# Edge batches of five tiles instead of four, partial sums in one go, and another order of the loads at the start

## The chip, the cores and the metric

The kernel runs on one core of a Trainium2 chip. The metric is the time of one execution on the device in microseconds. A core has five engines with queues of their own, which wait for one another only by semaphores: TensorE (PE in the profile; its weight loads are PEld), VectorE (DVE), ScalarE (ACT), GpSimd (POOL) and SyncE (SP). Transfers are issued by SP, ACT and POOL.

## What is computed

One message-passing layer on a graph of 1250 nodes and 40000 edges, sorted by destination, then a residual and a layer norm. Cut to what matters:

```python
x_j = x[src]; v_j = x_j[:, :384].reshape(E, 128, 3); s_j = x_j[:, 384:]
s_j = silu(s_j @ W1 + b1) @ W3 + b3
edge_basis = rbf * cutoff @ W2 + b2            # 20 waves of the edge's length
s1, s2, s3 = split(s_j * edge_basis)
msg = concat([v_j * s1[:, :, None] + s3[:, :, None] * edge_attr[:, None, :], s2])
x = x + segment_sum(msg, dst)                  # first pass
x_j = x[src]
v = U(v_j); v_V = V(v); h = silu(concat([norm(v_V), s_j]) @ Wu1 + bu1) @ Wu2 + bu2
msg = concat([v * s1, sum(v * s1 * v_V) + s3])
x = x + segment_sum(msg, dst)                  # second pass
out = layernorm(x_in + x)
```

In the second pass a message depends on the source node alone. So the kernel does it by nodes, with a matrix of counts (how many edges go from one node to another) in place of a second gather.

## The kernel before

**Tiles.** 128 edges are a tile; there are 313, in 80 batches (`batches`, `NT`): 76 of four tiles, then one of three and three of two. The edges stand in chunks of 512; four chunks make a group (`NGR` = 20), and a batch holds the same quarter of the four chunks of its group, so that the four tiles go to four different windows of 32 destination nodes.

**The head** (`gnn_resnorm`, L85 to L413). Node features are loaded in pieces: the scalar part by ACT's queue, the vector part by POOL's, small weights and the edges' fields by SP's. `turn_s`, `inner_layer` and `make_rows` make the ten blocks of `table1` (PE and ACT make the products, DVE multiplies the features in `table_row`, L611, SP stores the row, L616). The edges' fields are turned by PE (`by_tile`, L293). Then DVE checks by two reductions (L371) that every edge lies in its chunk's window; PE adds up the misses (L377), and all engines read the number and branch into `windowed` (L415, L416).

**The main loop** (`windowed`, the loop over `t` at L1730). A step `t` does, in this order of issue: `messages(t)`, in which DVE multiplies the gathered rows by the edge factors `eb` (L938, L940), makes `hot` (L870) and `spread` (L881) from columns that lie in `eb` too, runs the tasks of `amid`, and compares places in `make_pair` (L958); then the tasks of `first`; `add_messages(t-1)`, in which PE sums the messages into the group's bank `agg` (L974, L980); `count_links(t-1)` (PE, L1003); the tasks of `early`; `edge_factors(t+1)`, in which PE writes the next factors into `eb` (L928); `gather(t+3)`, one indirect DMA on POOL for each tile (L769), of which the first waits for these factors; then the tasks of `mid`, `late` and `dve`. Each engine works through its part of this order; it is written out by hand. There is one set of `eb`, so that the factors of a batch can be written only when DVE's `spread` has read those of the batch before. PSUM's banks are shared out so: four are `eb`, and one each is `agg`, `adj` (counts), `begun`, and `work`, which all short works share.

**The second pass** is worked into the same steps. A block of 128 nodes has its sums after eight steps (`begins`); its update takes ten steps more (`links_at`). From then on its rows can be multiplied by counts. A chain (b, begin, end) in `chains` is the part of output block b that comes from source blocks begin to end-1. `begin_out` does one source block per call (two matmuls of 512 columns, L1378), and the calls are spread over `early` and `late` tasks by `slots`. The sum stays in the bank `begun` until `copy_begun` takes it out (ACT, L1397). `cast_counts` makes the counts for a chain beforehand.

Of the kernel before, what the change touches and what calls it, by code (L numbers as in the profile page):

```python
# [11 lines left out]
F32 = mybir.dt.float32  # L12
# [34 lines left out]
PACK = 4096.0  # L47

# [16 lines left out]
def gnn_resnorm(  # L65
# [43 lines left out]
    )  # L109
    sh.n_nodes, sh.width, sh.n_edges, sh.NB, sh.tail = n_nodes, width, n_edges, NB, tail  # L110
# [22 lines left out]
    def load_edges(t, ap, per=1):  # L133

        flat = ap if per == 1 else ap.rearrange("e k -> (e k)")
        n = full * CHUNK * per
        nc.sync.dma_start(t[:full, :], flat[:n].rearrange("(c e) -> c e", e=CHUNK * per))
        if rest:
            nc.sync.dma_start(
                t[full : full + 1, : rest * per], flat[n:].rearrange("(o e) -> o e", o=1)  # L140
            )
# [9 lines left out]
    def load(engine, ap, shape, name):  # L151
        t = const.tile(shape, F32, name=name)
        engine.dma_start(t, ap)
        return t
# [15 lines left out]
    sh.nodes = const.tile([P, NB * width], F32, name="nodes")  # L170
# [12 lines left out]
    nc.gpsimd.memset(sh.src_r[unfilled:, :], 0.0)  # L183

    size = CPG * (V + 2 * C)
    sh.more = const.tile([P, 3 * size], F32, name="more")
# [20 lines left out]
    sh.b1_sb = load(nc.sync, b1.rearrange("(p o) -> p o", o=1), [C, 1], "b1_sb")  # L207
# [3 lines left out]
    sh.w3_sb = load(nc.sync, w3, [C, V], "w3_sb")  # L211
    load_outer(nc.sync, of_s)
    load_edges(dst_r, dst)
    load_edges(sh.src_r.bitcast(I32), src)


# [10 lines left out]

    row_i = front.tile([P, 1], I32)
    nc.vector.tensor_copy(row_i, part)
    nc.vector.tensor_scalar(row_i, row_i, -WIN, None, op0=ALU.bitwise_and)  # L230
    place = front.tile([P, 3], F32)
    nc.vector.tensor_copy(place[:, 2:3], row_i)
    place_row = front.tile([P, 1], F32, name="place_row")
    nc.vector.tensor_copy(place_row, row_i)
    nc.vector.scalar_tensor_tensor(
        place[:, 0:1], place[:, 2:3], float(SHARE - WIN) / WIN, part, op0=ALU.mult, op1=ALU.add
    )
    nc.vector.tensor_scalar(
        place[:, 2:3], place[:, 0:1], float(P - GSPAN), float(-P), op0=ALU.is_ge, op1=ALU.mult
    )  # L240
    nc.vector.scalar_tensor_tensor(
        place[:, 1:2], place[:, 0:1], float(GSPAN), place[:, 2:3], op0=ALU.add, op1=ALU.add
    )
    nc.gpsimd.memset(sh.wgt_r[unfilled:, :], 1.0)
    lane = numbers([P, P], [[1, P]], 0, 0, "lane")
    nc.vector.tensor_sub(place[:, 2:3], part, place_row)
    nc.vector.tensor_scalar(
        place[:, 2:3], place[:, 2:3], float(-N_RBF - 1), None, op0=ALU.add
    )
    nc.gpsimd.tensor_scalar(  # L250
        w2_sb[:, V:], lane[:, :CARRY], place[:, 2:3], None, op0=ALU.is_equal
    )
    half_n = numbers([P, N_RBF], [[1, N_RBF]], 1, 0, "half_n")
# [3 lines left out]

    nc.gpsimd.tensor_scalar(half_n, half_n, 0.5, None, op0=ALU.mult)
    sh.sel = const.tile([P, 2, P], F32, name="sel")
    for k in range(2):  # L260
        nc.gpsimd.tensor_scalar(sh.sel[:, k, :], lane, place[:, k : k + 1], None, op0=ALU.is_equal)

# [4 lines left out]
    )  # L267
    sh.basis = const.tile([P, TPC * CPG, FEAT], F32, name="basis")
# [80 lines left out]
    inner_layer(first_s[:, 2 * P :], (3, 4))  # L349
    part_bias(nc.vector, bias_f, slice(0, V))  # L350


    local_r = front.tile([NCP, CHUNK], F32)
# [1820 lines left out]
```

## Time and profile before

| | |
|---|---|
| Time, median of 3 runs | 478.65 us (477.8 to 480.88) |
| The profiled execution | 480.96 us |
| Its span, first to last instruction | 479.2 us |
| Mean granted clock of TensorE | 0.957 |
| Busy: PE / DVE / ACT / POOL | 402.6 / 427.8 / 375.3 / 334.9 us |
| Moved by DMA | 123.29 MB, 257 GB/s |

Busy time is that of instructions on the engine; issuing a transfer, waiting and branching are not in it. An instruction's duration includes its latency, so that two that follow each other on DVE overlap a little in the records; what one costs its engine is the distance between the starts of two. Matmuls are pipelined, and their ends are modelled. In a row of a timeline, what stands in brackets is the idle time of the engine before it and what ended it; "issue" means that the profile shows nothing else that it waited for.

### The profile page before, as it was taken

What the parts mean: (1) busy time and instruction counts of PE and PEld (TensorE: products, weight loads), DVE (VectorE), ACT (ScalarE), POOL (GpSimd) and SP (SyncE); (2) the same over time, 40 slices, a digit from 0 to 9 for tenths busy, and PEclk for the clock granted to TensorE, in tenths of its full rate; (3) what the DMA queues carried; (4) which work ended last, traced back from release to release, by engine and by line L of the source; (5) the groups of instructions that cost most, each with busy time, mean ns of one, the idle gap of its engine ahead of it and who ended that gap; (6) DMA issues with size and microseconds to landing.
All of it is one profiled execution on the core that took longest, in us unless ns stands there. A gap on an engine that the chain in (4) does not pass through costs nothing. (4 is left out here: it accounts for less than half of the span.)

```text
span 479.2 us, 11259 instructions
## 1 busy us (share of the span) xinstructions
PE 402.6 (84%) x4259; PEld 229.3 (48%) x4259; DVE 427.8 (89%) x675; ACT 375.3 (78%) x971; POOL 334.9 (70%) x364
## 2 busy tenths in 40 slices
PE   8645586878879778798889888989999999999992
PEld 6322243445445345444435544555555655555782
DVE  6569899999999899999999999999999999978584
ACT  4377846689869968877977897799899889967672
POOL 9267777777777777777777777777777777771530
PEclk9857979899999999989989999999999999999998
DMA  8887888788888888888888988888888888879024
GB/s 238 301 247 253 254 265 271 240 279 262 281 254 272 289 259 275 270 269 255 280 276 255 293 267 280 266 291 287 287 275 293 265 284 291 280 242 319 4 71 151
DMA packets 37810, 123.29 MB, mean 257 GB/s; under 512 B 7124, under 2 KB 9782, under 8 KB 37746
## 3 DMA queue, kind: packets, MB, share of 16 engines
q0 software_dynamic: 25568, 104.34, 69.0%
q1 hardware_dynamic: 10834, 17.35, 10.6%
q10 hardware_dynamic: 1344, 0.79, 0.5%
q8 instruction: 35, 0.57, 0.5%
q14 instruction: 29, 0.24, 0.2%
HBM read 112.94 MB, written 9.51 MB: 256 GB/s over the span
## 5 line engine op out<-in xcount | busy, mean ns | idle before, releaser
L769 POOL DMA_INDIRECT more<-table,src_i x189 | 184.6, 977 | 66.3 <-issue 48.1
L769 POOL DMA_INDIRECT nodes<-table,src_i x124 | 119.8, 966 | 37.8 <-issue 33.2
L903 ACT ACTIVATE one<-one,weight,src_f 128x128 f16<-128x128 f16 x313 | 128.5, 482 | 0.2
L928 PE MATMUL eb<-w_sb,basis_t 25*128 25x388 f32 x614 | 74.1, 551 | 54.3 <-DVE spread L881 43.9
L893 ACT ACTIVATE one<-number,low 128x128 f16<-128x128 f16 x313 | 99.8, 392 | 11.2 <-PE adj L1003 11.2
L940 DVE TENSOR_TENSOR more<-more,eb 128x1536 f32<-128x1536 f32 (+2 forms) x48 | 81.8, 1705 | 0.0
L938 DVE TENSOR_TENSOR more<-more,eb 128x1024 f32<-128x1024 f32 (+2 forms) x48 | 57.0, 1190 | 15.0 <-PE eb L928 8.2
L928 PEld LDWEIGHTS eb<-w_sb,basis_t 25*128 25x128 f32 x614 | 24.7, 187 | 76.5 <-DVE spread L881 63.7
L974 PE MATMUL agg<-more,hot 128*32 128x512 f32 x378 | 52.8, 624 | 0.0
L940 DVE TENSOR_TENSOR nodes<-nodes,eb 128x1536 f32<-128x1536 f32 x30 | 52.4, 1747 | 0.0
L980 PEld LDWEIGHTS agg<-more,spread 128*32 128x32 f32 x1134 | 33.5, 111 | 30.2 <-issue 29.6
L938 DVE TENSOR_TENSOR nodes<-nodes,eb 128x1024 f32<-128x1024 f32 x30 | 36.5, 1216 | 6.9 <-PE eb L928 4.0
L881 DVE TENSOR_TENSOR spread<-hot,eb 128x384 f32<-128x384 f32 (+1 forms) x74 | 40.4, 547 | 2.5
L980 PE MATMUL agg<-more,spread 128*32 128x128 f32 x1134 | 40.2, 273 | 0.0
L958 DVE TENSOR_TENSOR pair<-number,column 128x640 f16<-128x640 f16 (+1 forms) x81 | 38.5, 476 | 0.0
L1003 PE MATMUL adj<-pair,one 128*128 128x160 f16 x313 | 35.4, 235 | 0.3 <-DVE basis L827 0.3
L974 PE MATMUL agg<-nodes,hot 128*32 128x512 f32 x248 | 34.9, 619 | 0.0
L980 PEld LDWEIGHTS agg<-nodes,spread 128*32 128x32 f32 x744 | 22.7, 112 | 20.0 <-issue 19.6
L1003 PEld LDWEIGHTS <-one 128*128 128x128 f16 x313 | 21.6, 100 | 16.0 <-issue 13.5
L845 ACT COPY basis_t<-work 128x512 f32<-128x512 f32 x20 | 11.6, 580 | 22.5 <-PE work L840 22.5
L1378 PE MATMUL begun<-upper,cast 128*128 128x512 f32 x57 | 27.8, 487 | 0.0
L980 PE MATMUL agg<-nodes,spread 128*32 128x128 f32 x744 | 27.5, 277 | 0.0
(299 smaller groups left out, 697.3 us busy)
## 6 DMA issues: line engine op xcount, KB each, us to landing
table<-more SPq DMA_DIRECT2D x10, 320.0 KB
more<-table,src_i POOLq DMA_INDIRECT x189, 4.2
spilled<-begun SPq DMA_DIRECT2D x10, 256.0 KB
more<-spilled SPq DMA_DIRECT2D x2, 1280.0 KB
node_x<-in_x_dram SPq DMA_DIRECT2D x35, 64.0 KB
nodes<-table,src_i POOLq DMA_INDIRECT x124, 4.2
out_dram<-more SPq DMA_DIRECT2D x7, 256.0 KB
nodes<-in_x_dram POOLq DMA_DIRECT2D x2, 768.0 KB
```

Source lines behind the costliest of these rows:

```text
L769: got = nc.gpsimd.indirect_dma_start(out=rows_t[:n, j, :], out_offset=None, in_=sh.table1, in_offset=bass.IndirectOffsetOnAxis(ap=sh.src_i ...
L881: nc.vector.tensor_mul(spread[t][:m, js], hots[t][:m, js, None, :].to_broadcast(shape), carried(t, js, m)[:, :, :3, None].to_broadcast(shape),
L893: nc.scalar.activation(onehots[t][:, j, :], number[:, :P], AF.Abs, bias=low[:, e : e + 1])
L903: nc.scalar.activation(one, one, AF.Relu, scale=less[:, e : e + 1], bias=worth[:, e : e + 1])
L928: made = nc.tensor.matmul(made_in[t][:, j, : V + CARRY], turned[g][rows, i, :], sh.w2_sb[rows, :], start=True, stop=True,)
L938: nc.vector.tensor_mul(msg[:m, js, V:], msg[:m, js, V:], factors_of(t, js)[:m, :, C:V])
L940: nc.vector.tensor_mul(msg[:m, js, :V].rearrange("p t (k c) -> p t k c", k=3), msg[:m, js, :V].rearrange("p t (k c) -> p t k c", k=3), fac ...
L958: nc.vector.tensor_tensor(pair[:m, js, :].rearrange("p t (l h) -> p t l h", h=2), number[:m, : PARTS * WIN].rearrange("p (l h) -> p l h", ...
L974: nc.tensor.matmul(agg[j * WIN : (j + 1) * WIN, :], hots[t][:, j, :], msg[:, j, :width], start=(i == 0), stop=False, skip_group_check=True,)
L980: nc.tensor.matmul(agg[j * WIN : (j + 1) * WIN, c * C : (c + 1) * C], spread[t][:, j, c, :], msg[:, j, width:], start=False, stop=(i == la ...
L1003: nc.tensor.matmul(to[:, :, at : at + WIN], one[:m, j, :], pair[:m, j, :].rearrange("e (p n) -> e p n", n=WIN), start=(i == 0 and j == js[ ...
L1378: nc.tensor.matmul(acc, casts[a, b], rows[:, a, :], start=(start and a == first and k == 0), stop=(stop and a == end - 1 and k == 1),)
```

## The change

- **Packs of five.** Gathers, factors and messages work on packs of five tiles (`PACK_OF`, `packs`, `NK` = 65): 60 packs of five, then the tail's batches of four, three, two, two and two. `eb` has five banks. The sums of messages, the counts and all other tasks go on in steps of four tiles; `step_of(s)` gives the pack of a step, so that in steps 5, 10, 15 and so on no new pack begins. Five places of rows stand ready in place of 20 tiles' room; the fifth is a new one (`spare_slots`).
- **Begun sums at one go.** The bank `begun` goes to `eb`. A chain now runs all its blocks in one call, in the bank `work`, in `early` of the step that `steps_of` names (46, 48, 51, 53, 56, 61, 63, 68, 70, 71); the chain of block 8 runs in `late` of step 75. ACT copies it out in the same call.
- **The head.** The vector features go on SP's queue, behind the small weights and `dst`; `src` and `edge_weight` go on POOL's. The inner layer of blocks 5 to 8 comes ahead of the rows. The check of places stands between the rows of blocks 2 and 3, its sum behind row 5 and its copy behind row 6. The attribute load waits for the copy of `src_i` in place of the count. The places' numbers are worked out behind the bias.
- **Turns of the basis.** The tasks of `make_turns`, `make_basis` and `turn_basis` come one to three steps earlier.
- The last two blocks' `upper` and `lower` and the last casts take the spare place when the packs are done (`late_homes`), and `w1`, `w3` lie in the head's own room.

```diff
-    sh.w1_sb = load(nc.sync, w1, [C, C], "w1_sb")
+    sh.w1_sb = load(nc.sync, w1, [C, C], "w1_sb", front)
     load_inner(nc.scalar, of_s, 5)
     nc.scalar.activation(warm, warm, AF.Silu)
-    for b0 in (1, 5):
-        load_inner(nc.gpsimd, slice(0, V), b0)
-    load_outer(nc.gpsimd, slice(0, V))
     ...
-    load_outer(nc.sync, of_s)
-    load_edges(dst_r, dst)
-    load_edges(sh.src_r.bitcast(I32), src)
+    load_edges(nc.sync, dst_r, dst)
+    for b0 in (1, 5):
+        load_inner(nc.sync, slice(0, V), b0)
+    load_outer(nc.sync, slice(0, width))
+    load_edges(nc.gpsimd, sh.src_r.bitcast(I32), src)
+    load_edges(nc.gpsimd, sh.wgt_r, edge_weight)
...
     make_rows((1, 2))
-    inner_layer(next_s, (5, 6, 7, 8))
-    load_edges(sh.wgt_r, edge_weight)
-    make_rows((3, 4))
-    ...
     for k, op in enumerate((ALU.min, ALU.max)):
         nc.vector.tensor_reduce(ends[:, k : k + 1], local_r, AX.X, op)
     ...
+    make_rows((3, 4))
+    rest_s = turn_s((0, 9))
+    make_rows((5,))
+    nc.tensor.matmul(missed, misses, ones[:NCP, 0:1], start=True, stop=True)
+    inner_layer(rest_s, (0, 9))
+    make_rows((6,))
+    nc.vector.tensor_copy(missed_i, missed)
+    make_rows((7, 8, 0, 9))
...
+    def step_of(s):
+        return -(-4 * s // 5) if s < NT - SHORT else s - NT + NK
...
-        def begin_out(chain, a):
+        def begin_out(chain):
             b, begin, end = chain
-            if a == begin:
-                accs[b] = ps_sum.tile([P, BANK], F32, name="begun")
-            products(accs[b], b, a, a + 1, a == begin, a == end - 1)
-            if a == end - 1 and b < NB - 2:
-                copy_begun(b, chain)
+            acc = work()
+            products(acc, b, begin, end, True, True)
+            copy_begun(b, acc, chain)
...
+        steps_of = {
+            (4, 0, 4): 46, (0, 0, 4): 48, (3, 0, 4): 51, (5, 0, 5): 53, (2, 0, 5): 56,
+            (6, 0, 6): 61, (1, 0, 6): 63, (7, 0, 7): 71, (0, 4, 7): 70, (3, 4, 7): 68,
+        }
...
+            at(early, step, 8, begin_out, chain)
...
-        [eb] = new_banks("eb", [CPG])
+        [eb] = new_banks("eb", [PACK_OF])
...
+            k = step_of(s)
+            new = k not in begun_steps
+            if new and k < NK:
+                messages(k)
+            if s < NT:
+                run(amid, s)
+                make_pair(s)
...
             run(early, s)
+            if new and k + 1 < NK - 2:
+                made = edge_factors(k + 1)
...
+            if new and k + ahead < NK:
+                gather(k + ahead, made if k + ahead < NK - 2 else None)
```

## Rows read from the trace of the kernel before

**Rows 1.** The page, busy us (share of the span) and instructions of each engine

```profile
PE 402.6 (84%) x4259; PEld 229.3 (48%) x4259; DVE 427.8 (89%) x675; ACT 375.3 (78%) x971; POOL 334.9 (70%) x364
```

**Rows 2.** Windows: stretch, length, then busy us and instructions of each engine

```profile
100.00:250.00 150.00, 123.93 (x1467) 67.72 (x1462) 141.40 (x202) 126.65 (x333) 114.34 (x118) 0.98 0.86 270
300.00:400.00 100.00, 96.95 (x1083) 54.95 (x1081) 96.43 (x138) 89.00 (x231) 75.93 (x80) 1.00 0.87 281
```

**Rows 3.** Timeline of POOL: start us, us, engine line op out<-in, idle before it

```profile
26.35 1.09 POOL L769 DMA_INDIRECT more<-table,src_i  x1 [7.61 <-DVE turn L792]
...
29.02 0.95 POOL L769 DMA_INDIRECT more<-table,src_i  x1 [0.30 <-issue]
...
426.96 0.95 POOL L769 DMA_INDIRECT nodes<-table,src_i  x1 [0.30 <-issue]
```

**Rows 4.** The page's groups of instructions, the gathers: busy us, mean ns

```profile
L769 POOL DMA_INDIRECT more<-table,src_i x189 | 184.6, 977 | 66.3 <-issue 48.1
...
L769 POOL DMA_INDIRECT nodes<-table,src_i x124 | 119.8, 966 | 37.8 <-issue 33.2
```

**Rows 5.** Timeline of DVE, one batch and the start of the next

```profile
216.38 1.21 DVE L938 TENSOR_TENSOR more<-more,eb 128x1024 f32<-128x1024 f32 x1
217.51 1.75 DVE L940 TENSOR_TENSOR more<-more,eb 128x1536 f32<-128x1536 f32 x1
219.17 0.28 DVE L870 TENSOR_TENSOR hot<-lane,eb 128x128 f32<-128x128 f32 x1
219.49 0.55 DVE L881 TENSOR_TENSOR spread<-hot,eb 128x384 f32<-128x384 f32 x1
219.96 0.48 DVE L958 TENSOR_TENSOR pair<-number,column 128x640 f16<-128x640 f16 x1
...
221.36 1.21 DVE L938 TENSOR_TENSOR more<-more,eb 128x1024 f32<-128x1024 f32 x1
```

**Rows 6.** Waits (us, times, longest): PE from 100 to 250; PE, DVE 300 to 400

```profile
PE eb L928 <- DVE spread L881: 24.7, 23, 2.2
...
PE eb L928 <- DVE spread L881: 1.4, 6, 0.3
...
DVE nodes L938 <- PE eb L928: 1.3, 2, 0.7
DVE more L938 <- PE eb L928: 1.3, 3, 0.7
```

**Rows 7.** Windows of L1378 alone, then of L928 alone: PE, PEld busy

```profile
300.00:400.00 100.00, 22.47 (x63) 9.82 (x62) 1.00 0.87 281
...
300.00:400.00 100.00, 18.61 (x160) 6.25 (x160) 1.00 0.87 281
```

**Rows 8.** Timeline of the head, of DVE and POOL

```profile
4.58 0.15 DVE L247 TENSOR_SCALAR place<-place 128x1 f32<-128x1 f32 x1
...
7.26 0.55 DVE L329 TENSOR_TENSOR bias<-bias_f,bias 1x384 bf16<-1x384 f32 x1
10.30 1.27 DVE L611 TENSOR_TENSOR more<-nodes,pp 128x384 f32<-128x384 f32 x2 [2.49 <-DMA nodes<-in_x_dram]
...
19.38 3.11 DVE L611 TENSOR_TENSOR more<-nodes,pp 128x384 f32<-128x384 f32 x4 [0.20 <-ACT more L610]
...
24.34 0.15 DVE L378 CAST missed_i<-missed 1x1 int32<-1x1 f32 x1 [0.28 <-PE missed L377]
...
15.57 1.57 POOL L354 TENSOR_SCALAR local_r<-dst_r,share 80x512 f32<-80x512 int32 x1 [3.61 <-DMA dst_r<-in_dst_dram]
```

**Rows 9.** Timeline of PE, a chain's six products and the factors behind them

```profile
417.87 0.48 PE L1378 MATMUL begun<-upper,cast 128*128 128x512 f32 x1
418.18 0.39 PE L1378 MATMUL begun<-lower,cast 128*128 128x512 f32 x1
...
419.12 0.40 PE L1378 MATMUL begun<-lower,cast 128*128 128x512 f32 x1
419.44 0.93 PE L928 MATMUL eb<-w_sb,basis_t 25*128 25x388 f32 x8
```

More of the change, by code (lines that the diff above doesn't have):

```diff
@@ L47 @@
 PACK = 4096.0
+PACK_OF = 5
 REC = 8
@@ L267, in gnn_resnorm @@
     )
+    local_r = front.tile([NCP, CHUNK], F32)
+    nc.gpsimd.tensor_scalar(local_r, dst_r, share, None, op0=ALU.subtract)
     sh.basis = const.tile([P, TPC * CPG, FEAT], F32, name="basis")
@@ L845, in turn_basis, with clear_rest @@
             nc.scalar.copy(turned[g].rearrange("p i e -> p (i e)"), tp)
[L847 to L850 removed]
+        def clear_rest(k, tile, engine=nc.vector):
+            for q, n in enumerate(packs[k]):
+                m = lanes_of(n)
                 if m < P:
[L852 to L859 removed]
@@ L861, in make_hot, with carried @@
-        def make_hot(t):
-            g, i = batches[t]
-            hots[t] = pool.tile([P, CPG, WIN], F32, name="hot", bufs=3)
-            spread[t] = pool.tile([P, CPG, 3, WIN], F32, name="spread", bufs=3)
-            clear_rest(t, hots[t])
-            clear_rest(t, spread[t])
-            for js, n, m in runs(g, i):
+                    engine.memset(tile[m:, q], 0.0)
+        kept_apart = sh.carried.rearrange("p g t c -> p (g t) c")
+        def carried(k, qs, m):
+            first = packs[k][0]
+            if first < EPG:
+                return kept_apart[:m, first + qs.start : first + qs.stop, :]
+            return factors_of(k, qs)[:m, :, V : V + CARRY]
@@ L1067, in sum_block @@
                 blks[b] = (
-                    work() if b < NB - 1 else ps_sum.tile([P, BANK], F32, name="begun")
+                    work() if b < NB - 1 else ps_late[0].tile([P, BANK], F32, name="begun")
                 )
@@ L1146, in times_uv @@
             x_t = upd[b][0]
-            vv_p = work() if b < NB - 1 else ps_sum.tile([P, BANK], F32, name="begun")
+            vv_p = work() if b < NB - 1 else ps_late[0].tile([P, BANK], F32, name="begun")
             for i in range(3):
@@ L1580, in windowed @@
         assert len(row_order) == 10
-        for b, _, end in sorted(chains):
+        for b, _, end in row_order:
             begun[b] = end
-        units = [(chain, a) for chain in chains for a in range(*chain[1:])]
-        slots = (
-            (0, early), (0, late), (1, late), (2, early), (2, late), (3, early), (3, late),
-            (4, early), (4, late), (5, late), (6, late), (7, early), (7, late), (7, late),
-        )
-        after = 0
-        free_slots = [(8 * c + step, when) for c in range(3, NB) for step, when in slots]
```

401 lines of the change are left out of this document (216 added, 185 removed).

## The prediction

> **What bounds the kernel now.** I read the page first, for the shares: no engine is idle for long, and DVE leads with 89% [rows 1]. A share is an average over stages, so the stages come next. In the windows of the long middle, GpSimd issued 118 gathers in 150 us and 80 in 100 us, one per 1.27 and 1.25 us [rows 2]. The timeline of GpSimd shows why that is a limit: after each gather's 0.95 us stand 0.30 us of "issue", which no other engine ends, and then comes the next gather. The first starts at 26.35 us, the last ends at 427.91 [rows 3]; these 401.6 us hold the 313 gathers (189 and 124) [rows 4], 1.28 us each. With 1.25 us for each, 391 us would be the least. So nothing that leaves the number of gathers alone can shorten this stretch by more than some 10 us, and before the first gather lie 26.35 us, behind the last 51.3 us.
>
> DVE runs almost as full. One batch of four tiles on the timeline of DVE starts its pieces at 216.38, 217.51, 219.17, 219.49 and 219.96: 1.13 us for the scalar part, 1.66 for the vector part, 0.32 for `hot`, 0.47 for `spread`, 3.58 in all. With the smaller works behind them the next batch starts after 4.98 us [rows 5]; four gathers take 5.0. Both streams run at the same pace, within one per cent.
>
> The third engine is PE, and the views by stage differ here. PE waited 24.7 us for `spread` in the 150 us from 100, but 1.4 us in the 100 us from 300 [rows 6]. There the begun sums (L1378) have 22.5 us of PE and the edge factors 18.6 us, 0.93 for each of 20 batches [rows 7]. PE therefore has nothing left in that stage, and still DVE waited for its factors only 2.6 us [rows 6]: the units of the begun sums are small, and spread out so that each batch's factors come just in time.
>
> **The head.** The check of places (L371 to L378) runs behind the last table row: DVE ends the rows at 22.49 us (19.38 and 3.11), and the count of misses at 24.49 [rows 8]. After the change the check stands behind rows 1 and 2, so of these 2.0 us all but the last conversion (0.15) leaves the end, 1.85 us. It isn't free there: DVE still does the check between the rows, and I book 1.85 us for it. The rest of the gain is the features: the first row waited 2.49 us for them until 10.30 although the bias was ready at 7.81, and `local_r` waited 3.61 us for `dst_r` until 15.57 [rows 8]. Now `dst_r` goes ahead of the features on SP, and the features go on SP ahead of the table's stores, so every SP transfer that the rows need is queued before the first store. The ten small works on places (0.15 us each [rows 8]) move behind the bias, so a first row can start at 7.81 + 1.5 = 9.3. Ten rows at 0.81 us (four of them took 3.11 [rows 8], and a little for PE) and the check's 1.85 make 19.25 in place of 22.5: 3.25 us, and 1.85 for the check that no longer follows: 5.1 us. Both ends: if only the check's place counts, 1.9; if the rows follow faster, at 0.63 each, 6.9. I take 5.1, because each wait that goes has its row in the head. GpSimd's edge loads cost nothing: they stand before its constants, and it waited 3.61 us behind these. Without that cover they would delay `local_r` by their issue. The attribute load, now behind `src_i`, moves forward with it, and the inner layer of blocks 5 to 8, ahead of the rows, fills the time in which PE now waits for the bias.
>
> The Trainium skill says under "DMA: Bandwidth & Descriptors", section "Issuing engines are not separate DMA queues", that issuing on other engines saves the sequencer's time only, since all run on the same 16 DMA engines. By it the move to SP would bring nothing, and the head's term would be the 1.9 us. The rows of the head speak for more, by the order of the loads and not by their engine.
>
> **Five tiles at one go.** DVE does 61 batches of four instructions in place of 76. From 1024 to 1536 elements the time rose from 1.13 to 1.66 us, about 1.04 ns per element [rows 5]; for 1280 and 1920 elements that is 1.40 and 2.06. `hot` and `spread` come to 0.34 and 0.53 by their own two rows. Five tiles then take 4.33 us, 17.3 for twenty tiles in place of 17.9: 0.6 us less in five steps, 8.7 us over the kernel. While the gathers set the pace this is worth nothing, and I book it only where DVE waits otherwise (3.5 us in the thirty steps from 46 on). Bounds: 0 and 8.7. A pack also needs five gathers before DVE may begin, 1.25 us or, at the first steps of a pack, two gathers (2.5 us) later than now; it costs 0 to 2.5 us once, where the gathers stop being the limit; I take 1.2.
>
> The Trainium skill gives in "Perfetto Trace Analysis", section "Optimizing Scalar/DVE Operations", about 125 ns per DVE instruction on PSUM and says that grouping pays if the engine is saturated. For 60 instructions fewer that is an estimate of 7.5 us. The rows' 8.7 us are close to it; what the gathers leave of it is another matter.
>
> **The begun sums at one go.** This is the part that decides. The fifth tile takes the bank of the begun sums, so a chain now runs whole inside one step, in `early`, and `edge_factors` of the next pack is queued behind it on PE. DVE cannot begin that pack without all five tiles' factors, and the factors cannot be written before DVE's `spread` has read the last ones: PE can't work ahead. How long is a burst? In the timeline three blocks' six products start at 417.87 and 418.18, then every 0.235 us to 419.12, and the factors start at 419.44 [rows 9]: 1.57 us, so 2.04, 2.51, 2.98 and 3.45 for four, five, six and seven blocks.
>
> How much of that has cover? PE's other work per step, from 300 on: 96.95 less 22.47 and 18.61, over 20 steps, 2.8 us [rows 2, 7]. From 100 to 250 it is 123.9 less 27.4 for the factors (29.5 batches at 0.93), 3.3 us, in which the first begun sums are left. Five tiles' factors take 1.16. DVE has about 1.4 us per step besides the messages. In five steps there are four packs, so one interval between two factors holds two steps of PE's other work. Double interval (the burst in a step s with s mod 5 of 0 or 1): DVE 4.33 + 2 x 1.4 = 7.1 us, PE 1.16 + 2 x 2.8 (to 3.3) = 6.8 to 7.8. To spare: from +0.4 to -0.6. Single interval (s mod 5 of 2 to 4): DVE 5.7, PE 4.0 to 4.5, 1.3 to 1.75 to spare. DVE's 1.4 us behind `spread` are 0.2 more than the factors' 1.16; that comes on top. I take 0.3 and 1.75, nearer to the stage from 300, where most chains run.
>
> Chains at steps 46, 51, 56, 61 and 70 with 71 lie in double intervals: 2.04 + 2.04 + 2.51 + 2.98 + 5.02 less 5 x 0.3 make 13.1 us. Those at 48, 53, 63 and 68 lie in single ones: 0.3 + 0.75 + 1.25 + 0, 2.3. Together 15.4 us in which DVE stands before `eb`; with the two ends of PE's work (0.6 and 1.95 to spare, or -0.4 and 1.5) 13.3 to 19.7. GpSimd cannot make it good: the gather of pack k+3 waits for the factors of pack k+1, and from 300 on it has no faster pace than 1.25 us. If the cover is as large as a burst, it is 0. The work bank adds waits for ScalarE's copy; I book none, since the factors that follow a chain use another bank. The last chain (step 75) has the same ten products as its units had, in the same steps; none. The turns of the basis are the same instructions one to three steps earlier, and the late homes of two blocks are taken when the packs are done, some steps before anything writes them; both cost nothing as long as no engine waits for them, and half a microsecond, the length of one such instruction, where one does.
>
> **Sum.** Head -5.1, packs +1.2, stalls +15.4, DVE's saving in the same steps -3.5: +8.0 us. The profiled execution took 480.96 us, of it 479.2 of span, 2.3 over the median of 478.65. It would take 489.0; for the median that is 486.65, and I say 486.6. The ends: -1.9 + 2.5 + 19.7 - 3.5 = +16.8, 495.4; the lower end is the first rival's.
>
> **Rivals.** First, the bursts have cover, and it ends faster. For it: PE has less to do, as products took 0.35 us each in units (22.47 over 64) and take 0.235 in a burst. Against it: double intervals have no room, by both stages' rows. It decides from 2 us of spare per double interval on. Then the gathers set the pace from an earlier start, 478.65 - 5.1 = 473.5. Second, half of the stalls are covered, or the first rival comes with the head's 1.9 alone: 476 to 480. Third, DVE is the limit and the gathers follow it: 478.65 - 5.1 - 8.7 = 464.8. Against it stand gathers that follow one another with 0.30 us of issue and nothing else [rows 3]. It is the case in which the Trainium skill's rule on grouping would come out whole.
>
> **Chances.** Forecast 0.55 (480 to 494), first 0.25, second 0.15, third 0.05. The forecast's own range is 480 to 494; with the first two rivals the range is 472.5 to 495. A measurement of this kernel tells about 1% from no change, so 473.9 and 483.4 are the bounds. Faster: the third and half of the first, 0.2. Same: the other half, the second and the forecast's low edge, 0.3. Slower: 0.5.
>
> **What would show it.** The first gather at 21 us, not 26.35. Gathers 1.25 us apart to about 270 us; behind that, gaps of 1 us or more in front of a pack's first gather. DVE waits for `eb` of 2 to 4 us behind steps 46, 51, 56, 61 and 71, some 15 us in total against 2.6 in rows 6, and PE's rows of L1378 in ten blocks. Wrong would be: no such waits; PE waiting for `spread` in the same stretch; gathers without gaps to the end; or a last gather that ends less than 402 us behind the first.

## The result, and the profile after

The changed kernel takes 573.23 us (median of 4 runs, 569.09 to 575.78) against 478.5: 1.194 times as long, 95% interval 1.189 to 1.199. The forecast was 486.6, range 472.5 to 495. Slower was right; some 87 us are missing from it.

The profiled execution took 569.09 us, its span is 567.3 (before 479.2), the mean granted clock 0.902 (before 0.957). In two of the five groups of runs below the kernel before itself took 566 and 560 us, for a reason that no run here shows, and those runs are compared only with runs beside them.

The page after, busy us and instructions of each engine, to be read against [rows 1]: PE has 56 us more to do with as many instructions, ACT 14 us more, and all have a smaller share of the longer span.

```profile
PE 458.8 (81%) x4259; PEld 267.1 (47%) x4259; DVE 424.7 (75%) x615; ACT 389.3 (69%) x979; POOL 332.3 (59%) x362
```

Windows after (stretch, length, busy us of PE, PEld, DVE, ACT, POOL, then granted clock, DMA share, GB/s), against [rows 2]: 101 gathers in the first in place of 118, 63 in the second in place of 80. One gather per 1.49 us, then per 1.59. The first stretch ends before the first burst of begun sums, so something else came first.

```profile
100.00:250.00 150.00, 122.08 (x1266) 67.60 (x1262) 119.83 (x152) 110.43 (x286) 96.54 (x101) 0.91 0.74 229
300.00:400.00 100.00, 85.86 (x841) 50.03 (x836) 73.45 (x95) 75.57 (x190) 59.39 (x63) 0.94 0.71 221
```

The waits of DVE before `eb`, whole span (us, times, longest), after and then before: 69.8 us in place of 12.2.

```profile
DVE both L996 <- PE eb L987: 57.5, 26, 10.3
...
DVE spare_slots L996 <- PE eb L987: 12.3, 8, 4.4
```

```profile
DVE more L938 <- PE eb L928: 8.2, 12, 2.7
...
DVE nodes L938 <- PE eb L928: 4.0, 8, 0.7
```

**The ring.** Timeline after of one pack, DVE and then PE (start, us, engine, line). DVE's messages run from 212.72 to 217.19, 4.47 us. Then PE makes the next factors, 217.25 to 218.82, and before that DVE can't begin the next pack. In the quiet packs (k = 5 to 7, 10 and 11, 18 and 19 and others) one `spread` ends 6.13 us behind the other: 4.47 + 0.06 + 1.57 + 0.04 with the short ways from engine to engine. Before, the shortest distance is 3.67 + 0.06 + 0.93 + 0.07 = 4.73 for four tiles. For a tile that is 1.226 against 1.183. Both lie below the 1.25 us of a gather [rows 3], so that an undisturbed ring of five would still keep up with the gathers; but to spare are 0.12 us per pack in place of 0.27 us per batch.

```profile
212.72 1.49 DVE L996 TENSOR_TENSOR spare_slots<-spare_slots,eb 128x1280 f32<-128x1280 f32 x1 [1.02 <-PE eb L987]
214.13 2.15 DVE L998 TENSOR_TENSOR spare_slots<-spare_slots,eb 128x1920 f32<-128x1920 f32 x1
216.19 0.32 DVE L929 TENSOR_TENSOR hot<-lane,eb 128x160 f32<-128x160 f32 x1
216.54 0.65 DVE L939 TENSOR_TENSOR spread<-hot,eb 128x480 f32<-128x480 f32 x1
...
217.25 1.57 PE L987 MATMUL eb<-w_sb,basis_t 25*128 25x388 f32 x10 [0.92 <-DVE spread L939]
```

**A stall at a turn of the basis** (pack 13), timeline after of ACT, PE and DVE. ACT loads a table for the Sin, for which DVE stands 4.13 us in `make_basis` (L886), and another one behind it; its copy of `s` out of the work bank comes behind `distances` and `mark_sources`. PE stands 2.36 us before the transposes for that copy, and the sums of messages and the factors are queued behind them: factors at 138.84 for a `spread` that ended at 135.15.

```profile
127.82 1.28 ACT L865 ACT_TABLE_LOAD   x1
129.12 0.74 ACT L865 ACTIVATE turn<-turn 128x640 f32<-128x640 f32 x1
...
130.02 1.28 ACT L1266 ACT_TABLE_LOAD   x1
...
132.75 1.64 ACT L961 ACTIVATE one<-one,weight,src_f 128x128 f16<-128x128 f16 x4
134.29 0.25 ACT L1293 COPY s<-work 128x128 f32<-128x128 f32 x1
...
134.59 0.66 PE L899 MATMUL work<-ident,basis 128*128 128x128 f32 x4 [2.36 <-ACT s L1293]
135.17 1.89 PE L1031 MATMUL agg<-both,hot 128*32 128x512 f32 x8
136.82 1.53 PE L1038 MATMUL agg<-both,spread 128*32 128x128 f32 x24
...
138.84 1.57 PE L987 MATMUL eb<-w_sb,basis_t 25*128 25x388 f32 x10
...
129.89 0.49 DVE L886 TENSOR_TENSOR basis<-turn,adj 128x320 f32<-128x320 f32 x1 [4.13 <-ACT turn L865]
...
140.44 1.49 DVE L996 TENSOR_TENSOR spare_slots<-spare_slots,eb 128x1280 f32<-128x1280 f32 x1 [4.42 <-PE eb L987]
```

The windows on both sides of that wait. The granted clock falls to 0.57 behind it, and the two sums take 1.89 and 1.53 us; at 1.00, some microseconds earlier (128.04 and 128.92), they took 1.06 and 0.84.

```profile
131.00:135.00 4.00, 0.91 (x7) 0.71 (x6) 3.97 (x4) 3.52 (x11) 2.53 (x3) 1.00 0.88 296
135.00:139.00 4.00, 4.00 (x43) 2.01 (x45) 1.03 (x3) 2.37 (x7) 0.00 (x0) 0.57 0.32 99
```

**The longest stall** (the chain of step 61, six blocks), PE and DVE. Transposes wait 1.33 us for the work bank, the first product 1.72 us for ACT's copy of them; then 12 products start 0.43 us apart, where [rows 9] have 0.235; the granted clock is 0.50 from 417 to 422 us.

```profile
413.69 0.66 PE L899 MATMUL work<-ident,basis 128*128 128x128 f32 x4 [1.33 <-ACT vv L1215]
416.07 0.80 PE L1439 MATMUL work<-upper,cast 128*128 128x512 f32 x1 [1.72 <-ACT basis_t L904]
...
421.48 1.80 PE L987 MATMUL eb<-w_sb,basis_t 25*128 25x388 f32 x10
...
423.32 1.49 DVE L996 TENSOR_TENSOR both<-both,eb 128x1280 f32<-128x1280 f32 x1 [10.28 <-PE eb L987]
```

**The head after.** The first row waits for features until 11.67 us ([rows 8]: 10.30), blocks 0 and 9 reach PE at 15.14, the first gather starts at 27.59 ([rows 3]: 26.35), and the first messages wait for gathered rows.

```profile
4.20 0.96 SPq L439 DMA_DIRECT2D both<-in_x_dram  x2
...
11.67 1.24 DVE L611 TENSOR_TENSOR both<-both,pp 128x384 f32<-128x384 f32 x2 [1.44 <-DMA both<-in_x_dram]
...
15.14 0.76 PE L282 MATMUL xs<-ident,both 128*128 128x128 f32 x2 [3.34 <-DMA both<-in_x_dram]
...
27.59 1.10 POOL L828 DMA_INDIRECT both<-table,src_i  x1 [11.27 <-DVE vv L767]
...
38.45 1.49 DVE L996 TENSOR_TENSOR both<-both,eb 128x1280 f32<-128x1280 f32 x1 [4.20 <-DMA both<-table,src_i]
```

### The profile page after: what moved, and what is told of

The parts are those of the page before. It is cut to its first block, busy times and chain, and to the rows that moved or that the text cites. A ratio compares the mean times of both kernels' runs of the same rounds, so it can differ in the third digit from the quotient of the medians.

```text
span 567.3 us, 11205 instructions
## 1 busy us (share of the span) xinstructions
PE 458.8 (81%) x4259; PEld 267.1 (47%) x4259; DVE 424.7 (75%) x615; ACT 389.3 (69%) x979; POOL 332.3 (59%) x362
## 4 chain that ended last, share of the span: by engine, by line
DVE 28%; PE 25%; ACT 14%; issue 12%; POOL 10%; DMA 7%; DVEq 0%; POOLq 0%
PE eb L987 9%; DVE both L998 8%; POOL both L828 6%; DVE both L996 6%; DMA both<-table,src_i 5%; ACT one L961 4%; PE agg L1031 4%; DVE spread L939 3%; PE work L1439 3%; ACT one L951 2%; PE agg L1038 2%; POOL spare_slots L828 2%; DVE spare_slots L998 2%; PE adj L1061 2%; DVE spare_slots L996 2%
## 5 line engine op out<-in xcount | busy, mean ns | idle before, releaser
L828 POOL DMA_INDIRECT both<-table,src_i x253 | 246.2, 973 | 151.9 <-PE eb L987 71.1
L987 PE MATMUL eb<-w_sb,basis_t 25*128 25x388 f32 x614 | 102.0, 553 | 56.2 <-DVE spread L939 46.5
L996 DVE TENSOR_TENSOR both<-both,eb 128x1280 f32<-128x1280 f32 (+3 forms) x51 | 73.5, 1444 | 65.2 <-PE eb L987 57.5
L998 DVE TENSOR_TENSOR both<-both,eb 128x1920 f32<-128x1920 f32 (+3 forms) x51 | 106.3, 2085 | 0.0
L1031 PE MATMUL agg<-both,hot 128*32 128x512 f32 x506 | 92.0, 697 | 0.0
L1038 PEld LDWEIGHTS agg<-both,spread 128*32 128x32 f32 x1518 | 57.5, 122 | 48.5 <-issue 47.0
L828 POOL DMA_INDIRECT spare_slots<-table,src_i x60 | 57.9, 964 | 35.4 <-PE eb L987 18.4
L1038 PE MATMUL agg<-both,spread 128*32 128x128 f32 x1518 | 69.7, 297 | 0.0
L939 DVE TENSOR_TENSOR spread<-hot,eb 128x480 f32<-128x480 f32 (+3 forms) x59 | 37.7, 640 | 1.9
L1031 PE MATMUL agg<-spare_slots,hot 128*32 128x512 f32 x120 | 31.9, 746 | 0.0
L1038 PEld LDWEIGHTS agg<-spare_slots,spread 128*32 128x32 f32 x360 | 18.9, 127 | 12.6 <-issue 12.4
```

Source lines behind the costliest of these rows:

```text
L828: got = nc.gpsimd.indirect_dma_start(out=rows_k[:m, q, :], out_offset=None, in_=sh.table1, in_offset=bass.IndirectOffsetOnAxis(ap=sh.src_i ...
L939: nc.vector.tensor_mul(spread[k][:m, qs], hots[k][:m, qs, None, :].to_broadcast(shape), carried(k, qs, m)[:, :, :3, None].to_broadcast(shape),
L987: made = nc.tensor.matmul(made_in[k][:, q, : V + CARRY], turned[g][rows, i, :], sh.w2_sb[rows, :], start=True, stop=True,)
L996: nc.vector.tensor_mul(msg[:m, qs, V:], msg[:m, qs, V:], factors_of(k, qs)[:m, :, C:V])
L998: nc.vector.tensor_mul(msg[:m, qs, :V].rearrange("p t (k c) -> p t k c", k=3), msg[:m, qs, :V].rearrange("p t (k c) -> p t k c", k=3), fac ...
L1031: nc.tensor.matmul(agg[j * WIN : (j + 1) * WIN, :], hots[k][:, q, :], msgs[k][:, q, :width], start=(i == 0), stop=False, skip_group_check= ...
```

## The experiments

**What sets the pace, and which part costs what.** My new theory was the ring (DVE's messages, PE's next factors, DVE's next messages), with what stands late in it; rivals were the gathers' own pace, the bursts, and the turns. factors_again repeats in the kernel before the factors of each batch's first tile, as many matmuls as a fifth tile has:

```diff
+            if len(tiles(g, i)) == CPG:
+                j, rows = 0, slice(0, N_RBF + 1 + CARRY)
+                made = nc.tensor.matmul(made_in[t][:, j, : V + CARRY], ...)
```

> The kernel before, in which each batch of four tiles computes the factors of its first tile a second time (same values, same bank, same rows of the array), as the fifth tile of a pack does by its place. Theory 'ring': the factors take 1.57 instead of 0.93 us, 0.64 us more for each of 76 batches, 48.6 us; up to 19 us of it are hidden by DVE's small works, which now end 0.25 us behind the factors on average: 508 to 527 us. Rival 'gathers set the pace' (the reading on which the forecast rested; DVE and PE have cover): 478 to 483 us.

Measured: 507.09 us (479.11 beside it), just under the ring's 508 to 527. The factors with the two repeated matmuls end 1.56 us behind their first start, nearly as the ten do after:

```profile
208.07 0.93 PE L928 MATMUL eb<-w_sb,basis_t 25*128 25x388 f32 x8 [1.09 <-DVE spread L881]
208.82 0.81 PE L934 MATMUL eb<-w_sb,basis_t 25*128 25x388 f32 x2
```

So 0.63 us more of PE in each of 76 batches, 48 us, cost 28. One `spread` now ends 5.33 us behind the other in most batches (3.67 + 1.56 + 0.10), so here the ring sets the pace. It also shows that in the kernel before it did not: 20 of the 48 us were covered, 0.27 us per batch, the distance from the ring's 4.73 to the 5.0 us of four gathers. DVE's own work per batch, 4.98 us [rows 5], would cover as much; but gathers that were kept back by DVE would wait for factors, and before they hardly do. Their waits for factors, whole span, in before, factors_again and after (0.30 us of each is the "issue" of [rows 3]):

```profile
POOL more L769 <- PE eb L928: 2.3, 3, 1.1
```

```profile
POOL more L769 <- PE eb L934: 31.3, 38, 2.2
...
POOL nodes L769 <- PE eb L934: 19.2, 25, 1.5
```

```profile
POOL both L828 <- PE eb L987: 71.1, 24, 12.4
```

packs_of_four keeps all of the change but the fifth tile:

```diff
-PACK_OF = 5
+PACK_OF = 4
-                room = k % PACK_OF
-                first, t = (0, spare_slots) if room == PACK_OF - 1 else (room * PACK_OF, sh.slots)
+                first, t = k % 5 * PACK_OF, sh.slots
```

> The changed kernel with PACK_OF = 4: four tiles to a pack, four banks of eb, a new pack in every step; the new head, the earlier turns of the basis, the begun sums at one go in the work bank stay. Theory 'ring' (a pack costs DVE's messages plus PE's factors, one behind the other, since there is one set of eb; 4.47 + 1.57 + 0.1 us = 6.13 for five tiles after, 3.67 + 0.93 + 0.1 = 4.69 for four before, and what a double interval leaves uncovered comes on top): the factors fall back to 0.93 us, no interval holds two steps, and the time comes back to 478.5 plus at most the bursts of the forecast, 480 to 500 us. Rival 'bursts and early turns' (the sums at one go, the one work bank and the earlier turns make the loss, whatever the size of a pack): 540 us or more.

Measured: 533.87 us, ratio 1.114 (1.107 to 1.121). Neither theory: the fifth tile makes 39 us, and 55 are left. Three more steps back divide them:

```diff
@@ four_old_turns, on packs_of_four
-                at(early, base - 2, 5.5, make_turns, g, n, 3)
-                at(first, base, 1, turn_basis, g)
+                at(early, base + 1, 5.5, make_turns, g, n, 3)
+                at(first, base + 3, 1, turn_basis, g)
...
@@ four_own_bank, on four_old_turns
-            acc = work()
+            acc = ps_sum.tile([P, BANK], F32, name="begun")
```

> Packs of four as in the run before, and the tasks of the turns of the basis put back to the steps of the kernel before (make_turns from base - 3, make_basis at base + 2, turn_basis at base + 3). The new head and the begun sums at one go in the work bank stay. Theory 'turns': with packs of four 533.9 us were measured, and in that trace the factors come 2.4 to 4.1 us late once in every eight steps, PE standing in front of the turn's transposes for the work bank, with another 1.0 and 0.6 us in the steps behind; without them some 30 us go: 500 to 508 us. Rival 'sums at one go': the loss lies in the steps from 46 on, and little moves: 525 us or more.

> As four_old_turns, and the chains, still at one go, have a bank of their own again (packs of four leave one free) and don't share the work bank. Theory 'work bank': a chain at one go waits in PE's queue for ScalarE's copy of the short work before it, and the short works behind it for ScalarE's copy of the chain; with its own bank only the length of the bursts is left, and 8 to 20 us go against four_old_turns, to 483 to 495 us. Rival 'length of the bursts': the waits are the products themselves; within 5 us of four_old_turns.

before_new_head has the head of the changed kernel and the main loop of before.

> The kernel before with the head of the changed one (loads, order of the inner layer, check between the rows), all of the main loop as before. By the trace of the changed kernel the first gather starts 1.2 us later with this head (27.59 us), since SP issues the vector features at 4.2 us behind the small loads, where GpSimd issued them at 2.2: 479 to 481 us. By the forecast the head gains 1.9 to 6.9 us: 472 to 477 us.

Measured: four_old_turns 503.29, four_own_bank 494.06, before_new_head 482.34 us (ratio 1.0065, 1.0026 to 1.0103); the first two are as expected, the third is slower than either expectation. The parts, each step adding one, hold for this order of steps; no other was run. The stages are those between the ends of DVE's `spread` of batches 9, 44 and 74 (tiles 39, 179, 299, which end a pack of either size), from the traces (the traced run of after is the quickest of its four, so that its row adds up to 35 us of the 39):

| kernel | us | step | 9 to 44 | 44 to 74 | 74 to end |
|---|---|---|---|---|---|
| before | 478.7 | | 179.4 | 153.2 | 60.0 |
| before_new_head | 482.3 | head +3.6 | 178.0 | 153.6 | 59.8 |
| four_own_bank | 494.1 | sums at one go +11.7 | 178.9 | 163.6 | 60.8 |
| four_old_turns | 503.3 | in the work bank +9.2 | 177.5 | 173.1 | 62.0 |
| packs_of_four | 533.9 | early turns +30.6 | 191.0 | 189.1 | 62.3 |
| after | 573.2 | fifth tile +39.4 | 206.8 | 202.0 | 67.6 |

The row "sums at one go" holds all else of the new main loop too (rooms, casts, late homes); 10 of its 12 us lie in the stage of the chains, and the trace of four_own_bank shows them behind the chains: in eight of the ten steps that have one, the factors start 0.9 to 2.7 us behind DVE's `spread`, 14 us in sum. Step 56, where `spread` ended at 331.99:

```profile
332.06 0.55 PE L1438 MATMUL begun<-upper,cast 128*128 128x512 f32 x1
...
334.65 0.93 PE L986 MATMUL eb<-w_sb,basis_t 25*128 25x388 f32 x8
...
335.65 1.22 DVE L995 TENSOR_TENSOR both<-both,eb 128x1024 f32<-128x1024 f32 x1 [2.78 <-PE eb L986]
```

four_of_five leaves out the factors of the fifth tile and so divides the last row:

```diff
             for q, n in enumerate(packs[k]):
+                if q == 4 and k:
+                    continue
```

> The changed kernel, in which edge_factors leaves out the fifth tile of every pack but the first (its bank keeps old factors; the output is not the reference's). Theory 'ring': the factors of a pack take 0.93 instead of 1.57 us, and as they stand between DVE's spread and its next messages, 0.64 us of each of 60 packs go, 38 us: 530 to 540 us. Rival 'double intervals alone': only the packs with two steps count, and the other work takes its place: 560 us or more.

Measured: 540.72 us, 32.5 less than after. Its stages are 193.5, 191.2 and 66.1: nearly those of packs_of_four but for the tail. So the fifth tile's two extra matmuls make 32.5 of the 39 us, and the rival's 560 is refuted. But that grouping costs little besides is a balance of two terms. From batch 9 to 74 the shortest distances of `spread`, 5.53 us for five tiles here and 4.73 for four, add up to 287.6 and 307.5 us; the stages took 384.7 and 380.1. Packs of five with short factors save 20 us of ring and lose 25 to delays on top of it, among which the double intervals are.

**Bursts and turns with packs of five.** one_block multiplies the first block of each chain and leaves out the rest, turns_apart moves all the turns.

```diff
@@ one_block
-            products(acc, b, begin, end, True, True)
+            products(acc, b, begin, begin + 1, True, True)
@@ turns_apart
...
-                at(early, base - 2, 5.5, make_turns, g, n, 3)
-                at(first, base, 1, turn_basis, g)
+                at(early, base - 3, 5.5, make_turns, g, n, 3)
+                at(early, base, 1, turn_basis, g)
```

> The changed kernel, in which each of the ten chains of begun sums multiplies only its first block (37 blocks of 0.47 us, 17.4 us of PE, are left out; the output lacks these products). Theory 'bursts in the ring': the packs 41 to 57 whose factors came 2.0 to 11.2 us late (36 us in sum) lose most of that: 535 to 555 us. Rival 'bursts covered, the stalls are others': 565 us or more.

> The changed kernel with the Sin of the turns one step earlier, and turn_basis in early, behind the sums of messages, instead of first. Theory 'the earlier turns stand in the ring' (DVE waits in make_basis for ACT's Sin, PE waits in front of the transposes for the work bank, and the next factors are queued behind both; 3.5 us in each of some eight groups): 540 to 555 us. Rival 'double intervals' (two steps of small works between two packs are too much, whichever of them comes first): 563 us or more.

Measured: 569.14 and 570.96 us; both lie in the rivals' ranges. one_block leaves the waits for the work bank where they were (1.33 and 1.72 us at step 61, as after): the factors of packs 41 to 57 still come 28 us late in sum (36 after), pack 49's 4.6 us (10.97 after), and some others come later than after; the granted clock is 0.861. turns_apart wins 3.3 us from batch 9 to 44 and loses 6.0 from 44 to 74.

**What of the turns costs 31 us.** Three candidates: the transposes' place, the clock, the Sin.

four_turn_later and four_turn_at_3 move the transposes back (the second also moves one `make_basis` by a step), four_warm and four_warm_2 (one kernel) let PE work while it waits: `keep_busy(n)` issues n unused matmuls of 388 columns into the free bank.

```diff
@@ four_turn_later, four_turn_at_3, on packs_of_four
-                at(first, base, 1, turn_basis, g)
+                at(first, base + 3, 1, turn_basis, g)
@@ four_warm, four_warm_2, on packs_of_four
+                at(early, base - 1, 20, keep_busy, 2)
+                at(first, base, 0.9, keep_busy, 3)
```

> Packs of four (533.9 us), in which of the turns' tasks only turn_basis goes back, from first of step base to first of base + 3, where the kernel before has it; make_turns with its Sin and make_basis stay early. Theory 'transposes in front of the work bank': at base the transposes wait 2.1 us for ScalarE to copy out the factors of the block (task of late, base - 1), with the sums of messages and the next factors queued behind them; at base + 3 they do not: 502 to 512 us, as with all turns put back (503.3). Rival 'Sin and make_basis early' (DVE and ScalarE wait for each other): 525 us or more.

> Packs of four (533.9 us), all turns early; PE does two more matmuls of 388 columns into the free bank ahead of the factors of step base - 1 and three ahead of the transposes at base, where it waited 1.5 and 2.1 us (results unused). Theory 'half of such a stall is the clock': in the trace of packs_of_four the granted clock is 0.5 from 164.5 to 171.3 us, around such a wait, and transposes and sums of messages behind it take 4.55 us in place of 2.5; with PE busy the clock stays at 2.4 GHz and 2 us of each of eight such stalls go: 512 to 525 us. Rival 'the clock falls all the same, or the matmuls cost what they save': 530 us or more.

Measured: 615.11 and 619.65 us, where the kernel before took 566.13; ratios 1.085 and 1.093, with no packs_of_four beside them, so that they don't answer the question. In four_turn_later a `make_basis` overwrites values that the transposes still have to read, in four_turn_at_3 a `make_turns` overwrites what a `make_basis` still has to read; the work is the same, the values aren't.

> The same kernel as packs_of_four, for comparison on this chip. Where the kernel before takes 479 us: 532 to 537 us, 1.114 of it. Where it takes 566 us, by every theory less of the ratio, 1.08 to 1.10, since there DVE waits for rows as well.

> packs_of_four with turn_basis alone back in first of step base + 3 (and make_basis of the second group one step later, so that it stays behind it); make_turns with its Sin and the first make_basis stay early. Theory 'transposes in front of the work bank': 502 to 512 us where the kernel before takes 479. Rival 'Sin and make_basis early': 525 us or more.

> packs_of_four with two unused matmuls ahead of the factors of step base - 1 and three ahead of the transposes. Theory 'half of such a stall is the clock': 512 to 525 us where the kernel before takes 479. Rival 'the clock falls all the same, or the matmuls cost what they save': 530 us or more.

Measured: 535.02, 522.58 and 531.29 us (479.75 beside them). The place of the transposes is worth 12.4 us, between the two expectations; in the traces 9.8 lie from batch 9 to 44 (181.4 us) and 0.9 from 44 to 74 (188.3). The clock: 0.898 rises to 0.939, and of the stall at 163 to 172 us the windows show the cure, first packs_of_four_2, then four_warm_2:

```profile
163.00:167.00 4.00, 1.77 (x15) 0.93 (x15) 3.74 (x5) 3.97 (x11) 3.09 (x4) 1.00 0.82 249
167.00:172.00 5.00, 4.40 (x44) 2.37 (x48) 1.98 (x5) 2.70 (x9) 2.43 (x3) 0.66 0.88 296
```

```profile
163.00:167.00 4.00, 4.00 (x29) 2.42 (x33) 3.74 (x5) 2.76 (x9) 3.08 (x4) 1.00 0.89 277
167.00:172.00 5.00, 5.00 (x53) 2.20 (x56) 3.50 (x6) 4.87 (x13) 3.57 (x5) 1.00 0.85 270
```

From batch 9 to 44 that gives 9 us (191.2 to 182.1), as the theory wants; from 44 to 74, where the unused matmuls share PE's queue with the chains, the stage takes 3.4 us more (189.2 to 192.6). The median gains 3.7, so that the expected 512 to 525 is missed and the rival's range met: over the whole kernel the matmuls cost most of what they save.

The third candidate is in ACT's rows, first packs_of_four, then four_old_turns. With the early turns the Sin stands between the Sqrt (L1252) and the Silu (L1265) of an update and needs a table of its own; with the old ones it comes behind the Silu and loads none. There are 30 table loads of 1.28 us in place of 22.

```profile
156.12 1.28 ACT L1252 ACT_TABLE_LOAD   x1
...
160.41 1.28 ACT L864 ACT_TABLE_LOAD   x1
161.70 0.74 ACT L864 ACTIVATE turn<-turn 128x640 f32<-128x640 f32 x1
...
162.61 1.28 ACT L1265 ACT_TABLE_LOAD   x1
```

```profile
157.07 1.28 ACT L1265 ACT_TABLE_LOAD   x1
158.36 0.37 ACT L1265 ACTIVATE h_t<-work,bu_sb 128x128 f32<-128x128 f32 x1
```

four_sin_apart is packs_of_four with the first three lines and the Sin of turns_apart; four_turns_apart has its transposes too.

> packs_of_four (534 to 535 us) with make_turns one step earlier still, so that the Sin no longer stands between Sqrt and Silu of an update; transposes at first of step base as in packs_of_four. Theory 'table loads': eight loads of 1.28 us leave ScalarE, with the waits for the work bank behind them, and 10 to 20 us go: 515 to 525 us. Rival 'only the place of the transposes counts': 531 us or more.

> four_sin_apart, and turn_basis in early of step base, behind the sums of messages (the turns of turns_apart, with packs of four). If table loads and transposes add up, nearly all of the 31 us go: 503 to 512 us. Rival 'the transposes stand in front of the factors in early as well': within 4 us of four_sin_apart.

Measured: 604.04 and 636.57 us, where the kernel before took 559.71 (ratios 1.083 and 1.142). Side by side they show one thing: transposes in `early`, behind the sums of messages, cost 32.5 us more than in `first`. The short works behind them now wait for ACT's copy of the transposes, the chains 19.6 us (2.4 in four_sin_apart) and the sums of a block 27.4 us, all ahead of the next factors:

```profile
PE work L1127 <- ACT basis_t L903: 27.4, 7, 4.3
...
PE work L1438 <- ACT basis_t L903: 19.6, 4, 7.1
```

That fits turns_apart: there DVE's wait for the Sin in `make_basis` falls from 9.1 us to 0.5, and PE's for that copy rises from some 3 us to 12. What the table loads alone are worth stays open. The wait for the transposes' bank is also what the clock falls behind, so the two measured parts overlap, and 15 of the 31 us or more are neither. The Sin's loads are a candidate for them, not shown; the earlier `make_basis` and `bring_fades`, which four_old_turns put back too, are others.

**The head.** check_moved puts only the check of places between rows 5 and 6 of the kernel before; head_mixed has the new head with the vector features on GpSimd's queue again.

```diff
@@ check_moved, on the kernel before
     make_rows((5,))
     inner_layer(rest_s, (0, 9))
+    for k, op in enumerate((ALU.min, ALU.max)):
+        nc.vector.tensor_reduce(ends[:, k : k + 1], local_r, AX.X, op)
...
+    make_rows((6, 7))
+    nc.tensor.matmul(missed, misses, ones[:NCP, 0:1], start=True, stop=True)
@@ head_mixed, on before_new_head
+    for b0 in (1, 5):
+        load_inner(nc.gpsimd, slice(0, V), b0)
+    load_outer(nc.gpsimd, slice(0, V))
```

> The kernel before with one piece of the new head: the check of places stands between the table rows of blocks 5 and 6, where DVE waited 1.8 us and local_r has been ready since 17.1 us, its sum behind row 7 and its copy behind row 8; the loads stay. By the forecast's smallest term for the head 1.85 us go: 476 to 477.5 us against 478.7. Rival 'the last table row's way to memory sets the first gather, not the check': 478 to 480 us.

> The kernel before with the new head, but with the vector features on GpSimd's queue as in the kernel before, the scalar features of blocks 0 and 9 on SP directly behind dst, and the check between rows 4 and 5. Theory 'the features on SP made the head late' (issued at 4.2 us instead of 2.2, blocks 0 and 9 last, so that block 5's row waits behind their transposes): the 3.6 us that the new head cost go, and the check's 1.9 besides: 475.5 to 478 us. Rival 'the order of the inner layer or of the check cost it': 480 us or more.

> The kernel before with the check of places between the table rows of blocks 5 and 6, nothing else. In the trace of check_moved the first gather started at 25.12 us, 1.23 us before that of the kernel before (26.35), though the time was the same on that chip. Theory 'the head's gain reaches the end': 477 to 478 us against 478.7 (a ratio of 0.996 to 0.998). Rival 'the main loop takes it back': 478.5 us or more.

Measured: ratios 0.9998 (0.997 to 1.003), 1.0025 (0.999 to 1.006) and 1.0008 (0.998 to 1.004). Nothing is won. In check_moved_2 the gathers start 1.38 us earlier than in [rows 3], and the first messages start at 36.42 us, where the kernel before had 35.68; the wait is for rows:

```profile
24.97 1.09 POOL L771 DMA_INDIRECT more<-table,src_i  x1 [7.48 <-DVE vv L722]
...
36.42 1.22 DVE L940 TENSOR_TENSOR more<-more,eb 128x1024 f32<-128x1024 f32 x1 [5.38 <-DMA more<-table,src_i]
```

The earlier gathers bring DVE its rows no sooner; SP's small loads of the main loop are issued in the same microseconds, and whether they hold up the rows was not tried. No version here beats the kernel before.

## Why the forecast was wrong, point by point

**What bounds the kernel.** The forecast read 0.30 us of "issue" between gathers [rows 3] as GpSimd's own pace and 391 us as the least. For the kernel before that holds: its gathers waited 2.3 us for factors in the whole span, and from batch 9 to 74 it took 332.6 us, where 260 gathers at 1.25 us make 325. The error is that a second limit lay close below and stands in no sum: the first gather of a pack waits for factors, and these for DVE's `spread`, a ring of 4.73 us per batch, 307.5 us in the same stretch. DVE waiting little and PE waiting 24.7 us for `spread` [rows 6] are two sides of that ring: DVE's small works (some 1.3 us a batch) just covered the 0.93 us of factors. The forecast weighed each engine's work per interval against the other's, as if they ran side by side. After, the ring's shortest distance makes 52 x 6.13 = 318.8 of 408.8 us, still under the gathers; what broke the pace are 90 us of delays on top of it, in place of 25.

**Five tiles: booked at +1.2 - 3.5 us, measured +39.4.** DVE's 4.33 us are 4.47, nearly right, and a tile did get cheaper on DVE (0.894 us for 0.918). The failed term is PE's: 1.16 us for five tiles' factors, scaled from 0.93. A tile's factors use 25 rows of the array at the place of its chunk; four tiles of a batch have four places, and their matmuls start 0.01 us apart; the fifth has the place of the first, and its two start 0.33 us apart behind the others. Five take 1.57. By the ring that is 0.41 us per pack more than booked, 25 us in 60 packs, and it wasn't covered by DVE's 1.4 us behind `spread`, as booked: 4.47 + 1.57 us stand one behind the other, 6.13 with the ways between, against the 5.7 booked for DVE. Without the two matmuls 32.5 of the 39.4 us go (four_of_five); the rest is the balance named there.

The grouping rule of the Trainium skill ("Perfetto Trace Analysis", section "Optimizing Scalar/DVE Operations") would have given 7.5 us, by the estimate in the forecast. DVE's busy time fell by 3.1 [rows 1], its share from 89% to 75%: it stood before `eb`, was no longer saturated, and the rule's own condition failed.

**Begun sums: booked at 15.4 us.** The mechanism was right and the size near: 11.7 us with a bank of their own, 10 of them in the stage of the chains, with DVE standing before `eb` 22.4 us in place of 12.2. This was measured with packs of four; the part of the double intervals in it was not. "Slower" rested on this term alone, the measured time mostly on others. But "the work bank adds waits for ScalarE's copy; I book none" is wrong by 9.2 us: at step 61 the transposes and the first product each wait for a copy that ACT reaches behind other work (`mark_sources`, 1.63 us; `cast` and `distances`, 0.83 and 1.28), and the factors are queued behind the products. The bank in which the factors lie was beside the point; the queue counts.

**Turns of the basis: booked at nothing, or 0.5 us; measured 30.6.** The step listed the instructions and took their number for their price. What they were moved past was not looked at: a work bank that ACT empties late (12.4 us), and a Sin between two functions with other tables (price not shown). From batch 9 to 44, 9 us of the 13.5 went where PE was kept busy and the granted clock stayed up.

**The head: booked at -5.1 us, measured +3.6.** "A first row can start at 9.3" failed: 11.67. SP issues the features at 4.20 us behind the small weights and `dst`; GpSimd issued them at 2.20; and blocks 0 and 9 come last, with block 5's row behind their transposes. The forecast's lower term, 1.9 us for the check's place, failed as well: an earlier first gather doesn't bring the rows sooner.

The Trainium skill ("DMA: Bandwidth & Descriptors", section "Issuing engines are not separate DMA queues") says that another issuing engine saves only the time to issue. The trace agrees in that the move to SP won nothing. That it lost by the order on SP is read from these rows and not shown: head_mixed, with the features on GpSimd again, came out at 1.0025, before_new_head at 1.0065, and their intervals overlap.

**What was to show it.** "First gather at 21": 27.59. "1.25 us apart to about 270": 1.49 from 100 to 250. "DVE waits of some 15 us in total": 69.8, of which 44.1 from 300 to 510 us. The waits behind steps 46 to 71 are there, up to 10.28 us; the others came earlier and were not foreseen. All rivals lay below the forecast; none named the ring.

## What to carry to other kernels

When two engines hand one buffer back and forth, add up what each does between the handovers, and hold that ring against what sets the pace now: here 0.27 us per batch lay between them. Once the ring is the longer one, whatever is queued ahead of the handover, on either engine or on the one that empties a shared bank, is paid. Before scaling a group of small matmuls from four to five, look where they lie in the array. Before moving a step, list what the engine does on both sides of its new place, ACT's tables included.

## What was not expected of the hardware

Five matmuls of 25 rows take 1.57 us, four take 0.93: the fifth and its second pass, at the place of the first, add 0.32 us each. In the Trainium skill, "TensorEngine Tiling (Array Packing)", section "Key Properties", different tiles of the array work in parallel; the rows agree for four, which start 0.01 us apart, and show that the fifth waits.

Behind a wait of PE of 2.36 us the granted clock was 0.57 after (135 to 139 us) and 0.66 in packs_of_four_2 (167 to 172), 1.2 GHz for a part of them, and five unused matmuls kept it at 1.00. Not every such wait does it: in the kernel before, one of 2.11 us that ended at 76.9 us was followed by 1.00.
